# Attention scores in the scans' PSUM during a wait, and first expert products between the routing's steps

## The chip, the cores and the metric

The kernel runs on one core of one Trainium2 chip. The metric is the device time of one execution in microseconds (us), lower is better; the time of a kernel is the median of its runs.

## The reference

Four images of 32x32 pixels with 256 channels (1024 tokens each) pass through four layers. Cut to what matters here:

```python
# layer 0: norm, w_in to 512, depthwise 3x3 conv, gelu = x; then a selective scan, N = 64 states per channel
dA = exp(dtt[:, :, None] * A)                          # over the tokens of an image, one after the other
h  = dA * h + (dtt * xt)[:, :, None] * Bt[:, None, :]
y  = einsum('bdn,bn->bd', h, Ct)                       # then norm, w_out, residual
# layer 1: 1x1, grouped 3x3 and 1x1 convolution with batch norm and relu, residual
# layer 2: t + attention(norm(t)): 8 heads of 32; tokens see each other where edge_index has an edge
scores = where(mask, Q @ K.T / sqrt(32), -inf); attended = softmax(scores) @ V   # @ Wo, residual, norm
#          then t + mixture of 8 experts (hidden 256) on x = norm(t), which adds x itself:
probs  = softmax(x @ router);  weights = top2(probs) / their sum
out    = x + sum over e of weights[:, e] * (gelu(x @ w1[e] + b1[e]) @ w2[e] + b2[e])
# layer 3: t + gated scan(norm(t)): 512 channels, 16 states, the same recurrence
#          then t + mixture of 8 experts (hidden 512) on x = norm(t), top 2 without renormalisation
```

## The kernel before, in words

**The scans.** The two scan layers are cut into 1280 units of 128 partitions (channel and state) by 1024 tokens. `scans()` (line 351) emits them in the order of `SCANS`: layer 0 of image 0, layer 0 of image 1, layer 3 of image 0, and so on; the last three are layer 0 of image 3, written (0,3), then (3,2) and (3,3). A scan of layer 0 has 256 units, one of layer 3 has 64; each falls into four blocks `d` of 128 channels. One unit needs, under these names:

- `load`: SyncE loads of the row of time steps, broadcast into `dA` (2 DMAs with 64 states, 8 with 16);
- `decay`: ScalarE's exp over `dA`;
- `first`: two TensorE products that spread the inputs over the states into PSUM (`ps_rep`);
- VectorE's multiply of `ps_rep` by B (TENSOR_TENSOR), then the scan itself (TENSOR_TENSOR_SCAN into `h`);
- GpSimd's multiply of `h` by C, and per two units `pair`: eight TensorE products that sum over the states (`ps_y`).

`chunk(k)` brings the inputs of a new block (`S`, loaded from `parts` in DRAM) twelve units ahead (`AHEAD`); `chunks_ahead` may put it off until five units ahead (`LATEST`), and then calls `need`, which advances the other work until the block's `parts` are there.

**The stages.** Everything else is a list of generators: `front` b (up to the scan of layer 0), `middle` b (`back0`: the end of layer 0; layer 1; `attention`; `moe(2, ...)`; `front3`: the projections ahead of the scan of layer 3), `last` b (`back3`, `moe(3, ...)`, output). `run()` (line 535) advances the running stage by at most two steps after each half of a unit, and only while a hand-made meter of engine costs (`Metered`) says that no engine's sum is ahead of VectorE's. Where `need` advances, there is no such limit, and nothing of the scans is emitted meanwhile. The order in which instructions are emitted is each engine's order: no scheduler rearranges it, and an instruction that waits holds all behind it on its engine. Scan (3,3) is the one that waits: its first block needs all of `middle` 3, which may only begin when (0,3) is done. At that point unit 1210 is finished, and unit 1211 stands behind the wait.

**PSUM.** The scans have tag `x` (two buffers of two banks, for `ps_rep`) and `y` (one bank). The stages have tags `s` (two banks) and `acc` (one); `ps()` deals these three out in turn.

**Pipes.** `pipe` (line 179) puts steps of successive items behind one another in one emission order:

```python
    for tick in range(len(items) + len(steps) - 1):
        for s in reversed(range(len(steps))):
            if 0 <= tick - s < len(items):
                steps[s](items[tick - s])
                if cut and s:
                    yield cost
        yield cost if tick < len(items) else 0.5
```

So the later step of an older item is emitted ahead of the first step of the next one.

**Attention.** `heads` (line 1302) works on two heads and 512 queries. For each of eight blocks of 128 keys, `scores` makes two tiles `ps_sc` of 128x512 (six products: two of queries and keys, two of `mT`, a shift that is added, two of the mask with an identity), then two exps into `p`; `values` takes four products out of `p` into `ps_at` (two with the values, two with ones for the sums). An image has eight such calls, in two halves `nh` with four pairs of heads `hp` each. After a half come the division, `projected` and `normed`.

**Experts.** `moe` (line 1412): norm, transposes (`ps_tr`), logits `ps_lg`, then `route` on VectorE: largest logit, exp on ScalarE, sum, division, the best and second best expert; its result is `cw`, one weight per token and expert. `cw` is transposed (`ps_ct`), copied, multiplied by the second biases (`ps_b2`, written ps_b in the profile) and added to `tb`. Then the experts: a pipe with `one` (a product `ps_h`, or `ps_e`) and `two` (the Gelu of `ps_h` into `h_m`, or the accumulation of `ps_e` times `cw` into `tb`). `KH` is the number of hidden blocks of 128: 2 in layer 2, 4 in layer 3. ScalarE's functions live in tables, so an exp after a Gelu is preceded by a table load (ACT_TABLE_LOAD).

All instructions of these functions are recorded at one helper line (L124 of the meter), so the profile tells them apart by their tiles.

Of the kernel before, what the change touches and what calls it, by code (L numbers as in the profile page):

```python
# [7 lines left out]
F32 = mybir.dt.float32  # L8
BF16 = mybir.dt.bfloat16
I32 = mybir.dt.int32  # L10
AF = mybir.ActivationFunctionType
ALU = mybir.AluOpType
# [4 lines left out]
P = 128  # L17
NB = 4
L = 1024
TB = L // P  # L20
C = 256
# [3 lines left out]
NEXP = 8  # L25
# [16 lines left out]
AHEAD = 12  # L42
LATEST = 5
# [89 lines left out]
class Hybrid:  # L133
# [217 lines left out]
    def scans(self, mp, psum):  # L351
# [7 lines left out]
        nc = self.nc  # L359
        units = []  # L360
# [5 lines left out]
            ]  # L366
        chunks, rows, waiting = {}, {}, []
        state = {}
        y = None

        def chunk(k):
# [22 lines left out]
                )  # L394
            chunks[scan, d] = S

        def chunks_ahead(k):

            if k + AHEAD < len(units) and units[k + AHEAD][2:] == (0, 0, 0):
                waiting.append(k + AHEAD)  # L400
            while waiting:
                scan, d = units[waiting[0]][:2]
                if waiting[0] - k > LATEST and ("parts", *scan, d) not in self.ready:
                    break
                chunk(waiting.pop(0))

        def load(k):
            if k >= len(units):
# [70 lines left out]
        decay(1)  # L479
        first(0)  # L480
        for k in range(len(units) + 4):
            chunks_ahead(k)
            load(k + 4)
            first(k + 1)
            decay(k + 2)
            if k < len(units):
                a, inp = state.pop(k)
                B, Cm = rows[units[k][0]]
                nc.vector.tensor_tensor(inp, inp, B, ALU.mult)
            yield  # L490
            if k < len(units):
                h = mp.tile([P, L], F32, tag="h", name="h", bufs=5)
                nc.vector.tensor_tensor_scan(h, a, inp, 0.0, ALU.mult, ALU.add)
                nc.gpsimd.tensor_tensor(h, h, Cm, ALU.mult)
                state[k] = h
            if k % 2 == 1 and 2 <= k < len(units) + 2:
                pair(k - 2)
            yield

    def need(self, scan, d):  # L500
# [34 lines left out]
    def run(self):  # L535

        self.done, self.ready = set(), set()
        self.todo, self.stage, self.wait = list(STAGES), None, None
        nc, tc = self.nc, self.tc
        with tc.tile_pool(name="scan", bufs=1) as mp, tc.tile_pool(  # L540
            name="scps", bufs=1, space=PSUM
# [760 lines left out]
    def heads(self, fp, raw, sums, qT, kT, v, maskT, mT, nh, hp):  # L1302

        nc = self.nc
        qs = slice(nh * 512, (nh + 1) * 512)
        c, at = hp // 2, 64 * (hp % 2)
        acc = self.psum.tile([P, 512], F32, tag="acc", name="ps_at", bufs=1)
        got = {}  # L1310

        def scores(kb):
            two = [self.psum.tile([P, 512], F32, tag="s", name="ps_sc", bufs=2) for _ in range(2)]
            rows = [slice(at + 32 * i, at + 32 * i + 32) for i in range(2)]
            for i in range(2):
                nc.tensor.matmul(
                    two[i], lhsT=kT[rows[i], c, kb * P : (kb + 1) * P], rhs=qT[rows[i], c, qs],
                    start=True, stop=False,
                )
            for i in range(2):  # L1320
                nc.tensor.matmul(
                    two[i], lhsT=self.onesb[rows[i], :], rhs=mT[rows[i], c, qs],
                    start=False, stop=False,
                )
            for i in range(2):
                nc.tensor.matmul(
                    two[i], lhsT=self.identb, rhs=maskT[:, kb, qs], start=False, stop=True
                )
            got[kb] = p = fp.tile([P, 2, 512], F32, tag="p", name="p", bufs=3)
            for i in range(2):  # L1330
                nc.scalar.activation(p[:, i, :], two[i], AF.Exp)

# [8 lines left out]
                    start=(kb == 0), stop=(kb == TB - 1), tile_position=(0, 32 * i),  # L1341
                )

        yield from self.pipe(range(TB), scores, values, cost=1.3, cut=True)
        nc.scalar.copy(raw[at : at + 64, c, :], acc[:64, :])
        nc.scalar.copy(sums[at : at + 64, c, :], acc[64:, :])

# [64 lines left out]
    def moe(self, which, b, tb):  # L1412

        nc, tc, a = self.nc, self.tc, self.a
# [4 lines left out]
        KH = hidden // P  # L1419
        with tc.tile_pool(name=f"m{which}{b}", bufs=1, side="right") as op:  # L1420
# [11 lines left out]
            with tc.tile_pool(name=f"mg{which}{b}", bufs=1, side="right") as gp:  # L1432
# [5 lines left out]
                for j in range(TB):  # L1438
                    for k in range(2):
# [1 line left out]
                            ps[:, j, :], lhsT=xT[:, k, j * P : (j + 1) * P],  # L1441
                            rhs=self.router[which][:, k, :], start=(k == 0), stop=(k == 1),
                        )
                yield 3.0
                if which == 2:
                    nc.vector.tensor_copy(lg, ps)
                else:
                    nc.vector.tensor_tensor(
                        lg, ps, self.gb.unsqueeze(1).to_broadcast([P, TB, NEXP]), ALU.add
                    )  # L1450
                yield 0.5
                if which == 2:
                    for j in range(0, TB, 2):
                        tj = tb[:, j : j + 2, :]
                        nc.gpsimd.tensor_tensor(tj, tj, xn[:, j : j + 2, :], ALU.add)
                        yield 0.6
                yield from self.route(gp, lg, cw, which == 2)

                cT = gp.tile([NEXP, L], F32, name="cT")

                def turn(g):
                    ps = self.ps("ps_ct")
                    for k in range(4):
                        nc.tensor.transpose(
                            ps[:NEXP, k * P : (k + 1) * P], cw[:, 4 * g + k, :], self.ident
                        )
                    nc.scalar.copy(cT[:, g * 512 : (g + 1) * 512], ps[:NEXP, :])

                yield from self.pipe(range(2), turn, cost=0.8)
                got = {}  # L1470

                def last(j):
                    got[j] = ps = self.ps("ps_b2", (P, 2, C))
                    for i in range(2):
                        m = 2 * j + i
                        nc.tensor.matmul(
                            ps[:, i, :], lhsT=cT[:, m * P : (m + 1) * P], rhs=self.b2[which],
                            start=True, stop=True,
                        )

                def add(j):
                    tj = tb[:, 2 * j : 2 * j + 2, :]
                    nc.vector.tensor_tensor(tj, got.pop(j), tj, ALU.add)

                yield from self.pipe(range(TB // 2), last, add, cost=1.0)

            hidden_of = {}
            got = {}

            def one(item):  # L1490
                kind, e, g, i = item
                we1, we2 = weights[e]
                if kind == "h":
                    if i == 0:
                        hidden_of[e, g] = op.tile([P, KH, 512], F32, tag="h", name="h_m", bufs=2)
                        if g == 1 and e + 1 < NEXP:
                            weights[e + 1] = expert_weights(e + 1)
                    got[item] = ps = self.ps("ps_h")
                    self.mm(
                        ps, lambda k: we1[:, k, i * P : (i + 1) * P], xT, 2,  # L1500
                        slice(g * 512, (g + 1) * 512),
                    )
                    return
                h = hidden_of[e, g]
                got[item] = ps = self.ps("ps_e", (P, 2, C))
                for s in range(2):
                    m = 2 * i + s
                    for f in range(KH):
                        nc.tensor.matmul(
                            ps[:, s, :], lhsT=h[:, f, m * P : (m + 1) * P], rhs=we2[:, f, :],  # L1510
                            start=(f == 0), stop=(f == KH - 1),
                        )

            def two(item):
                kind, e, g, i = item
                if kind == "h":
                    nc.scalar.activation(
                        hidden_of[e, g][:, i, :], got.pop(item), AF.Gelu,
                        bias=b1[:, e * KH + i : e * KH + i + 1],
                    )  # L1520
                    return
                ps = got.pop(item)
                for s in range(2):
                    m = 4 * g + 2 * i + s
                    nc.vector.scalar_tensor_tensor(
                        tb[:, m, :], ps[:, s, :], cw[:, m, e : e + 1], tb[:, m, :],
                        ALU.mult, ALU.add,
                    )

            items = []  # L1530
            blocks = [(e, g) for e in range(NEXP) for g in range(2)]
            for n in range(len(blocks) + 1):
                if n < len(blocks):
                    items += [("h", *blocks[n], i) for i in range(KH)]
                if n:
                    items += [("o", *blocks[n - 1], i) for i in range(2)]
            yield from self.pipe(items, one, two, cost=2.6 if which == 2 else 3.4)

    def route(self, gp, lg, cw, renorm):

# [277 lines left out]
```

## Time and profile before

| | |
|---|---|
| runs | 6815.66, 6822.12, 6823.56 us; median 6822.12 |
| profiled execution | 6818.64 us; its span 6816.9 |
| mean granted TensorE clock | 0.828 |
| busy | PE 5387.2 us (79%), DVE 5225.0 (77%), POOL 3651.6 (54%), ACT 3449.8 (51%) |
| scans on VectorE | 1280 multiplies of 1213 ns mean, 1280 scans of 2285 ns |
| GpSimd's multiply | 1280 of 2372 ns |
| ACT_TABLE_LOAD | 495 of 1283 ns |
| DMA | 937.44 MB, 137 GB/s over the span |

The profile is one execution, taken by the hardware profiler. PE is TensorE's products, PEld its weight loads, DVE is VectorE, ACT ScalarE, POOL GpSimd, SP SyncE. A row of digits cuts the span into 40 slices of 170 us, each digit the busy tenths of a slice. A timeline row has the start in us, the length, the engine, the operation, output<-input, the shape, and in brackets the idle time before it and the instruction that ended it; "x4" joins neighbours of one kind. Times inside the span are counted from its start.

### The profile page before, as it was taken

How to read it: one execution, taken by the hardware profiler on the slowest of the kernel's cores; microseconds unless marked ns; L12 is line 12 of the kernel's file. 1: busy time of each engine (PE TensorE's matmuls, PEld its weight loads, DVE VectorE, ACT ScalarE, POOL GpSimd, SP SyncE). 2: the span in 40 equal slices, each digit the busy share in tenths (PEclk: the TensorE clock that was granted, in tenths of full speed). 3: DMA queues.
4: the chain of work that ended last, by engine and by line, in shares of the span. 5: the costliest groups of instructions: out<-in, count | busy, mean ns of one | idle time of the engine just before them, and what ended most of it. 6: DMA issues, size and time to landing. Idle time of an engine off the chain costs nothing. (4 is left out here: it accounts for less than half of the span.)

```text
span 6816.9 us, 65916 instructions
## 1 busy us (share of the span) xinstructions
PE 5387.2 (79%) x20320; PEld 2164.2 (32%) x20320; DVE 5225.0 (77%) x4486; ACT 3449.8 (51%) x4152; POOL 3651.6 (54%) x1801
## 2 busy tenths in 40 slices
PE   6558778579797568979689679798698687967979
PEld 3003213122242022234145222243253222523556
DVE  8778988988798987889889977798899861247411
ACT  2426666445476334557568345477485443245411
POOL 0876786755457655555856555557666540054200
PEclk8558779689798578979789689798698789877989
DMA  2556665754365665446756655366666640146321
GB/s 72 147 144 161 178 173 154 194 138 119 102 169 162 182 156 143 115 120 177 192 144 163 178 150 129 103 161 169 171 170 178 155 117 7 45 134 148 84 62 34
DMA packets 394235, 937.44 MB, mean 138 GB/s; under 512 B 83220, under 2 KB 165728, under 8 KB 392224
## 3 DMA queue, kind: packets, MB, share of 16 engines
q1 hardware_dynamic: 391696, 930.53, 51.3%
q8 instruction: 172, 2.82, 0.2%
q0 software_dynamic: 2128, 2.13, 0.2%
q14 instruction: 239, 1.96, 0.1%
HBM read 842.59 MB, written 93.95 MB: 137 GB/s over the span
## 5 line engine op out<-in xcount | busy, mean ns | idle before, releaser
L124 POOL TENSOR_TENSOR h<-h,rows 128x1024 f32<-128x1024 f32 x1280 | 3032.7, 2372 | 1995.8 <-DVE h L124 1649.5
L124 DVE TENSOR_TENSOR_SCAN h<-dA,ps_rep 128x1024 f32<-128x1024 f32 x1280 | 2925.3, 2285 | 238.9 <-issue 105.6
L124 DVE TENSOR_TENSOR ps_rep<-ps_rep,rows 128x1024 f32<-128x1024 f32 x1280 | 1552.9, 1213 | 289.0 <-PE ps_rep L124 288.8
L124 ACT ACTIVATE dA<-dA,A_L_conv_A_log 128x1024 f32<-128x1024 f32 x1024 | 1153.5, 1145 | 727.9 <-DMA dA<-dt 673.5
L124 PE MATMUL ps_rep<-S,spread_L_conv_A_log 96*128 96x512 bf16 x2048 | 765.6, 465 | 743.6 <-DVE h L124 710.4
L124 PE MATMUL ps_y<-h,collect_L_conv_A_log 128*32 128x512 f32 x4096 | 802.2, 761 | 95.5 <-POOL h L124 93.5
L124 PE MATMUL ps_h<-xTm,we 128*128 128x512 f32 x1536 | 719.0, 607 | 3.8 <-ACT h_m L124 2.2
L124 PE MATMUL ps_e<-we,h_m 128*128 128x256 f32 x3072 | 702.3, 381 | 8.1 <-ACT h_m L124 6.4
L124 ACT ACT_TABLE_LOAD x495 | 635.1, 1283 | 74.8 <-PE ps_h L124 44.3
L124 PEld LDWEIGHTS <-spread_L_conv_A_log 96*128 96x128 bf16 x2048 | 161.5, 103 | 1523.6 <-DVE h L124 1220.7
L124 PEld LDWEIGHTS ps_e<-we,h_m 128*128 128x128 f32 x3072 | 581.3, 190 | 155.4 <-issue 45.7
L124 ACT ACTIVATE p<-ps_sc 128x512 f32<-128x512 f32 x512 | 277.8, 594 | 549.9 <-PE ps_sc L124 537.4
L124 DVE SCALAR_TENSOR_TENSOR tb<-ps_e,cw,tb 128x256 f32<-128x256 f32 x512 | 220.6, 474 | 404.3 <-PE ps_e L124 404.3
L124 ACT ACTIVATE h_m<-ps_h,cols 128x512 f32<-128x512 f32 x384 | 260.7, 687 | 473.6 <-PE ps_h L124 470.9
L124 ACT ACTIVATE dA<-dA,A_L_attn_A_log 128x1024 f32<-128x1024 f32 x256 | 293.3, 1148 | 384.8 <-DMA dA<-dt 342.8
L124 PE MATMUL ps_at<-p,v 128*32 128x512 f32 x1024 | 374.6, 610 | 64.6 <-ACT p L124 53.8
L124 PEld LDWEIGHTS ps_h<-xTm,we 128*128 128x128 f32 x1536 | 291.7, 193 | 341.4 <-issue 294.2
L124 PE MATMUL ps_rep<-S,spread_L_attn_A_log 96*128 96x512 bf16 x512 | 184.4, 449 | 195.2 <-DVE h L124 177.1
L124 PE MATMUL ps_sc<-qT,kT 32*128 32x512 f32 x1024 | 295.2, 649 | 44.8 <-ACTq L1234 26.0
L124 PE MATMUL ps_at<-p,ones 128*32 128x512 f32 x1024 | 272.1, 610 | 0.0
L124 PEld LDWEIGHTS ps_y<-h,collect_L_conv_A_log 128*32 128x32 f32 x4096 | 107.4, 119 | 492.4 <-POOL h L124 243.3
L124 PE MATMUL ps_cv<-pad,diag 128*128 128x512 f32 x576 | 260.4, 593 | 0.0
(306 smaller groups left out, 4945.8 us busy)
## 6 DMA issues: line engine op xcount, KB each, us to landing
dA<-dt SPq DMA_DIRECT2D x2048, 256.0 KB
dA<-dt SPq DMA_DIRECT2D x2048, 64.0 KB
we<-in_L_ffn_W_dram SPq DMA_DIRECT2D x64, 512.0 KB
parts<-parts SPq DMA_DIRECT2D x64, 384.0 KB
S<-parts SPq DMA_DIRECT2D x96, 256.0 KB
dt<-sp_r SPq DMA_DIRECT2D x64, 256.0 KB
y<-yo SPq DMA_DIRECT2D x128, 128.0 KB
y_back<-y SPq DMA_DIRECT2D x64, 256.0 KB
```

The lines of the kernel that those rows point to most:

```text
L124: return got(*args, **kw)
```

## The change

It has two parts.

*Heads during the wait.* `chunks_ahead(k)` now returns True where the block's parts are not there. In that case `first(k + 1)` is left out at its usual place, unit k's multiply and scan are emitted first, and then `chunks_ahead(k, True)` waits with `self.alone` set, followed by `first(k + 1)`. A call of `heads` that begins while `self.alone` is set takes its score tiles from the scans' PSUM (tag `x`: both tiles of a block in one buffer, `ps_sx`), computes one exp of 128x1024 in place of two of 128x512, and its pipe has an empty step between scores and values, so that the values of a block are emitted after the scores of two blocks later.

*Routing.* In `moe`, all between `ps_lg` and the experts becomes a generator `routing()`. After each of its yields, one tick of the experts' pipe is emitted, for the first `2 * KH` ticks: eight in layer 3, four in layer 2. `one` and `two` are as they were.

```diff
@@ scans
-        def chunks_ahead(k):
-            if k + AHEAD < len(units) and units[k + AHEAD][2:] == (0, 0, 0):
+        def chunks_ahead(k, late=False):
+            if not late and k + AHEAD < len(units) and units[k + AHEAD][2:] == (0, 0, 0):
                 waiting.append(k + AHEAD)
             while waiting:
                 scan, d = units[waiting[0]][:2]
-                if waiting[0] - k > LATEST and ("parts", *scan, d) not in self.ready:
-                    break
+                if ("parts", *scan, d) not in self.ready:
+                    if waiting[0] - k > LATEST:
+                        break
+                    if not late:
+                        return True
+                    self.alone = True
                 chunk(waiting.pop(0))
+                self.alone = False
+            return False
...
         for k in range(len(units) + 4):
-            chunks_ahead(k)
+            waits = chunks_ahead(k)
             load(k + 4)
-            first(k + 1)
+            if not waits:
+                first(k + 1)
             decay(k + 2)
...
             if k % 2 == 1 and 2 <= k < len(units) + 2:
                 pair(k - 2)
+            if waits:
+                chunks_ahead(k, True)
+                first(k + 1)
             yield
@@ heads
+        alone = self.alone
...
-            two = [self.psum.tile([P, 512], F32, tag="s", name="ps_sc", bufs=2) for _ in range(2)]
+            if alone:
+                both = self.scan_psum.tile([P, 2, 512], F32, tag="x", name="ps_sx", bufs=2)
+                two = [both[:, i, :] for i in range(2)]
+            else:
+                two = [self.psum.tile([P, 512], F32, tag="s", name="ps_sc", bufs=2) for _ in range(2)]
...
+            if alone:
+                nc.scalar.activation(p, both, AF.Exp)
+                return
             for i in range(2):
                 nc.scalar.activation(p[:, i, :], two[i], AF.Exp)
...
-        yield from self.pipe(range(TB), scores, values, cost=1.3, cut=True)
+        if alone:
+            yield from self.pipe(range(TB), scores, lambda kb: None, values, cost=1.3)
+        else:
+            yield from self.pipe(range(TB), scores, values, cost=1.3, cut=True)
@@ moe
+                def routing():
+                    yield 3.0
...
+                    yield from self.route(gp, lg, cw, which == 2)
...
+                    yield from self.pipe(range(TB // 2), last, add, cost=1.0)
...
-            yield from self.pipe(items, one, two, cost=2.6 if which == 2 else 3.4)
+                experts = self.pipe(items, one, two, cost=2.6 if which == 2 else 3.4)
+
+                ahead = 2 * KH
+                for cost in routing():
+                    yield cost
+                    if ahead:
+                        ahead -= 1
+                        yield next(experts)
+            yield from experts
```

More of the change, by code (lines that the diff above doesn't have):

```diff
@@ L368, in scans @@
         state = {}
+        self.scan_psum = psum
         y = None
@@ L538, in run @@
         self.todo, self.stage, self.wait = list(STAGES), None, None
+        self.alone = False
         nc, tc = self.nc, self.tc
@@ L1324, in scores @@
                 )
+            got[kb] = p = fp.tile([P, 2, 512], F32, tag="p", name="p", bufs=3)
             for i in range(2):
@@ L1328, in scores @@
                 )
-            got[kb] = p = fp.tile([P, 2, 512], F32, tag="p", name="p", bufs=3)
+            if alone:
+                nc.scalar.activation(p, both, AF.Exp)
+                return
             for i in range(2):
@@ L1443, in moe @@
                         )
[L1444 to L1465, printed above, removed]
-                        )
-                    nc.scalar.copy(cT[:, g * 512 : (g + 1) * 512], ps[:NEXP, :])
-                yield from self.pipe(range(2), turn, cost=0.8)
@@ L1470, in moe @@
-                got = {}
[L1472 to L1478, printed above, removed]
-                        )
-                def add(j):
-                    tj = tb[:, 2 * j : 2 * j + 2, :]
-                    nc.vector.tensor_tensor(tj, got.pop(j), tj, ALU.add)
@@ L1485, in moe @@
[L1485 to L1511, printed above, removed]
-                        )
@@ L1514, in two @@
[L1514 to L1536, printed above, removed]
-            yield from self.pipe(items, one, two, cost=2.6 if which == 2 else 3.4)
+                def routing():
+                    yield 3.0
+                    if which == 2:
+                        nc.vector.tensor_copy(lg, ps)
+                    else:
+                        nc.vector.tensor_tensor(
+                            lg, ps, self.gb.unsqueeze(1).to_broadcast([P, TB, NEXP]), ALU.add
+                        )
+                    yield 0.5
+                    if which == 2:
+                        for j in range(0, TB, 2):
+                            tj = tb[:, j : j + 2, :]
+                            nc.gpsimd.tensor_tensor(tj, tj, xn[:, j : j + 2, :], ALU.add)
+                            yield 0.6
+                    yield from self.route(gp, lg, cw, which == 2)
+                    cT = gp.tile([NEXP, L], F32, name="cT")
+                    def turn(g):
+                        ps = self.ps("ps_ct")
+                        for k in range(4):
+                            nc.tensor.transpose(
+                                ps[:NEXP, k * P : (k + 1) * P], cw[:, 4 * g + k, :], self.ident
+                            )
+                        nc.scalar.copy(cT[:, g * 512 : (g + 1) * 512], ps[:NEXP, :])
+                    yield from self.pipe(range(2), turn, cost=0.8)
+                    got = {}
+                    def last(j):
+                        got[j] = ps = self.ps("ps_b2", (P, 2, C))
+                        for i in range(2):
+                            m = 2 * j + i
+                            nc.tensor.matmul(
+                                ps[:, i, :], lhsT=cT[:, m * P : (m + 1) * P], rhs=self.b2[which],
+                                start=True, stop=True,
+                            )
+                    def add(j):
+                        tj = tb[:, 2 * j : 2 * j + 2, :]
+                        nc.vector.tensor_tensor(tj, got.pop(j), tj, ALU.add)
+                    yield from self.pipe(range(TB // 2), last, add, cost=1.0)
@@ new lines, in moe, with one @@
+                hidden_of = {}
+                got = {}
+                def one(item):
+                    kind, e, g, i = item
+                    we1, we2 = weights[e]
+                    if kind == "h":
+                        if i == 0:
+                            hidden_of[e, g] = op.tile([P, KH, 512], F32, tag="h", name="h_m", bufs=2)
+                            if g == 1 and e + 1 < NEXP:
+                                weights[e + 1] = expert_weights(e + 1)
+                        got[item] = ps = self.ps("ps_h")
+                        self.mm(
+                            ps, lambda k: we1[:, k, i * P : (i + 1) * P], xT, 2,
+                            slice(g * 512, (g + 1) * 512),
+                        )
+                        return
+                    h = hidden_of[e, g]
+                    got[item] = ps = self.ps("ps_e", (P, 2, C))
+                    for s in range(2):
+                        m = 2 * i + s
+                        for f in range(KH):
+                            nc.tensor.matmul(
+                                ps[:, s, :], lhsT=h[:, f, m * P : (m + 1) * P], rhs=we2[:, f, :],
+                                start=(f == 0), stop=(f == KH - 1),
+                            )
@@ new lines, in two @@
+                def two(item):
+                    kind, e, g, i = item
+                    if kind == "h":
+                        nc.scalar.activation(
+                            hidden_of[e, g][:, i, :], got.pop(item), AF.Gelu,
+                            bias=b1[:, e * KH + i : e * KH + i + 1],
+                        )
+                        return
+                    ps = got.pop(item)
+                    for s in range(2):
+                        m = 4 * g + 2 * i + s
+                        nc.vector.scalar_tensor_tensor(
+                            tb[:, m, :], ps[:, s, :], cw[:, m, e : e + 1], tb[:, m, :],
+                            ALU.mult, ALU.add,
+                        )
@@ new lines, in moe @@
+                items = []
+                blocks = [(e, g) for e in range(NEXP) for g in range(2)]
+                for n in range(len(blocks) + 1):
+                    if n < len(blocks):
+                        items += [("h", *blocks[n], i) for i in range(KH)]
+                    if n:
+                        items += [("o", *blocks[n - 1], i) for i in range(2)]
+                experts = self.pipe(items, one, two, cost=2.6 if which == 2 else 3.4)
[5 more added lines that the diff above has]
+                        yield next(experts)
```

## The prediction

> **What bounds the kernel now.** I read the page first: engine totals and slices.
>
> ```profile
> span 6816.9 us, 65916 instructions
> ...
> PE 5387.2 (79%) x20320; PEld 2164.2 (32%) x20320; DVE 5225.0 (77%) x4486; ACT 3449.8 (51%) x4152; POOL 3651.6 (54%) x1801
> ...
> DVE  8778988988798987889889977798899861247411
> ```
>
> VectorE (the scans: 1280 units of a 1.21 us multiply and a 2.29 us scan) carries the program for 32 of 40 slices; then its digits fall to 1 and 2. What bounds that end is read from windows cut at its events: image 3's last five head pairs (their first ends its predecessor's copy at 5607.14), the rest of its middle stage, the last 69 scan units, the rest of image 2's last experts, and image 3's last stage.
>
> ```profile
> 5440.00:5608.00 168.00, 140.38 (x660) 41.24 (x659) 116.46 (x73) 77.45 (x107) 87.28 (x42) 0.90 0.51 130
> 5608.00:5768.00 160.00, 137.68 (x656) 34.85 (x652) 11.40 (x19) 53.52 (x99) 7.55 (x6) 1.00 0.00 1
> 5768.00:6048.00 280.00, 234.53 (x696) 134.19 (x697) 61.23 (x163) 95.17 (x146) 34.67 (x28) 0.89 0.15 50
> 6048.00:6380.00 332.00, 239.04 (x862) 106.99 (x861) 266.59 (x217) 172.85 (x182) 191.07 (x94) 0.75 0.63 162
> 6380.00:6515.00 135.00, 129.27 (x468) 86.76 (x464) 17.51 (x40) 25.14 (x36) 2.25 (x1) 0.99 0.11 34
> 6515.00:6817.00 302.00, 261.87 (x904) 176.48 (x904) 42.74 (x113) 53.35 (x82) 14.81 (x12) 0.89 0.17 51
> ```
>
> Columns: length, then PE, PEld, DVE, ACT, POOL busy, granted clock, DMA share, GB/s. In the second row VectorE works 11 of 160 us: scan (3,3) waits for this attention, so every microsecond here moves the end by one. The timeline of one key block shows what TensorE waits for:
>
> ```profile
> 5645.90 1.13 PE L124 MATMUL ps_sc<-qT,kT 32*128 32x512 f32 x4
> ...
> 5646.87 0.38 PE L124 MATMUL ps_sc<-mT,onesb 32*128 32x512 bf16 x2
> 5647.18 0.61 PE L124 MATMUL ps_sc<-maskT,identb 128*128 128x512 bf16 x2
> 5647.67 1.08 ACT L124 ACTIVATE p<-ps_sc 128x512 f32<-128x512 f32 x2 [2.80 <-PE ps_sc L124]
> ...
> 5648.32 1.10 PE L124 MATMUL ps_at<-p,v 128*32 128x512 f32 x3 [0.53 <-ACT p L124]
> 5648.80 0.11 PEld L124 LDWEIGHTS ps_at<-p,v 128*32 128x32 f32 x1 [0.35 <-ACT p L124]
> ...
> 5649.79 1.13 PE L124 MATMUL ps_sc<-qT,kT 32*128 32x512 f32 x4
> ```
>
> Scores, exp and values run one after the other, 3.89 us a block. TensorE waits twice: for the first head's exp (to 5648.32) and for the second's (5648.80). The other place is the chain of waits in the last routing:
>
> ```profile
> 6567.22 6.64 PE ps_lg L124 x32
> ...
> 6573.88 0.24 DVE lg L124
> ...
> 6579.36 1.86 PE ps_ct L124 x8
> 6581.23 7.12 PE ps_b L124 x16
> 6588.35 15.49 PE ps_h L124 x32
> ```
>
> TensorE stands still for the 5.5 us of VectorE's steps and comes back slow: 32 ps_h take 15.49 us, 16 of them later 6.87 us, so 1.75 us is start-up, about four instructions at 0.85 instead of 0.43.
>
> **The change part by part.** My sum is against the profiled execution, 6818.64 us (its span of 6816.9 and 1.7 around it). That is 3.5 below the median of 6822.12, inside the three runs' own spread, so I correct nothing for it.
>
> *Heads in the scans' PSUM.* The wait is raised once, for scan (3,3): image 3's last five pairs, 40 blocks. In the built order their values follow the scores of two blocks later, and one exp of 128x1024 replaces two of 128x512. So the values' input is ready. Step by step from the timeline: scores 0.97 (5645.90 to 5646.87), mT 0.31, mask 0.44 (5566.29 to the next product at 5566.73), values 0.99. That last is the nearest row, ps_y, same shape (128*32, eight instructions):
>
> ```profile
> 6335.73 0.43 PE ps_rep L124 x2
> 6336.16 0.99 PE ps_y L124 x8
> ```
>
> Sum 2.71, so 1.18 saved a block, 40 x 1.18 = 47. ScalarE's exp (two were 1.08; the 128x1024 decay takes 1.15) fits under 2.71; were TensorE faster than that, it would be the bound. Given back: the last values of a pair wait some 0.35 for their exp (5 x 0.35 = 1.8), and in pair (1,2) the copies of the sums wait behind a table load, two small activations and four of 0.52 (about 2). **-43.** Bounds: only the recorded 0.53 goes (21), or nothing is given back (48). A rule speaks against the 47: the Trainium skill, TensorEngine Tiling (Array Packing), Key Properties, says that a change of tiling mode, not just of tile, drains TensorE, and mask to values is such a change, twice a block. By it the 0.53 may be drain; if all of it stayed the part would give 26, with the second wait alone 20. But ps_rep to ps_y above is the same change from full columns to 32-column tiles, and ps_y starts with no gap and takes 0.99 with its drain. I take the row.
>
> *Scan unit 1211 ahead of the wait.* Its multiply and scan (3.5 us) move from behind the stretch into its idle VectorE, its eight dA loads too (8 x 0.46 on SP). first(1212) is late next, but needs only 0.43 to 1.0 us while VectorE still has sp_x work. **-3.5** (0 to -6).
>
> *First products between the routing steps.* Eight for the last experts (KH 4), four for the middle ones.
> Tail (image 3): in the built order seven products stand before ps_ct. From the end of ps_lg: first product cold 3.4, six more 10.3 (4 x 0.43 each), ps_ct half 0.5, eighth 1.7, ps_ct 0.5, ps_b at full clock half of 7.12, 3.6: about 20.5. Now 6573.86 to 6603.84 is 30.0. The routing's exp now queues behind one Gelu and two table loads (3.4 + 0.7 + 1.3: at 5.7 instead of 0.8), cw is ready near 10, still before 13.7. **-9.5** (-4 to -11).
> Image 3's middle experts: only four products, three Gelus ahead of the exp on ScalarE. Products end at 8.6; exp at 3.4 + 1.7 + 1.7 + 0.7 + 1.3 + 0.3 = 9.2; five more us of VectorE: ps_ct at 14.3 instead of 6.3. ps_e starts at 14.3 + 1.8 + 7.1 = 23.3 instead of 24.15, and cold (1.7). **+1** (-3 to +3): the idle only changes place. Here a second rule counts: the Trainium skill, ScalarE: Activation LUTs, What ACT_TABLE_LOAD costs, gives about 1283 ns and a drain of about 1380. The profile's 495 loads have mean 1283, and at 6243.12 a decay starts as the load from 6241.83 ends: no drain. By the rule this routing costs 1.4 more; the whole built order has twenty more loads, 26 us of ScalarE by the row, 53 by the rule, nearly all beside VectorE's work.
> Image 2's last experts (scan units 1243 to 1247): VectorE idle 51 - 36.24 = 14.8 in 6205 to 6256, mostly for ps_rep and ps_b behind cold products. I take 3 off; and the stage stands one unit further at the last scan, a fifth of a 13.8 us expert half, 2.8. **-6** (-12 to +4).
> The five routings earlier: VectorE idles 10.6 + 10.3 + 11.0 + 12.4 + 12.1 = 56 in the same windows; the products now sit where TensorE waited for cw. No row shows the new mixture. Best, half of it goes (-28); worst, half of the added loads is exposed (+13). I take **-8**, near the middle.
> Moved with them: the second expert's two weight loads (0.4 us each on SP), now ahead of some dA loads. Their buffer is free, so they block none. Gpsimd's tb adds keep their place among its h multiplies. The fourth product needs the first one's PSUM, freed by its Gelu at 4.2. Behind the waiting exp on ScalarE stand the next decays, needed two units later by a scan.
>
> Sum: -43 - 3.5 - 9.5 + 1 - 6 - 8 = -69, so **6750 us**.
>
> **The rivals.**
> A, the drain stays: heads save 20 instead of 43, **6773**. For it the rule and the changes of mode; against it ps_y's 0.99.
> B, the routings give more: TensorE stays at full clock through ps_ct and ps_b and half of the 56 us goes: 20 more, **6730**. For it the granted clock of 0.56 to 0.68 there; against it that in the middle experts the four products are used up before the steps begin.
> C, slower, by ScalarE's order in the six routings under the scans: r_sm on VectorE waits for the exp, that for Gelus (3 x 3 in the middle experts, 3 x 1 in the last: 12), these for products that stand behind ps_rep, which waits for VectorE's scan. Price at most 3.4 + 0.7 + 2 x 1.28 + 0.26 = 6.9 each, 83 us, in place of the -8: **6841**. It eats the other gains (61) from 5.1 us a Gelu. Against it: the built order puts two scan units between lg and r_mx, and ScalarE waited 7 to 9 us for lg there.
> D, that the change does nothing, is excluded for the heads by the built order (40 exps of 128x1024); that gains and stalls cancel stays: about 6818.
>
> **How the numbers follow.** 0.2% (13.6 us) is about what a measurement of this kernel can tell from no change. Forecast 65% (6725 to 6772), A 16%, B 12%, C 4%, D 3%. The range of 6715 to 6785 leaves out C, D and the far ends of A and B. Faster 0.93 (forecast, A, B), same 0.03, slower 0.04.
>
> **What would show it.** In the profile after: blocks of ps_sx with 2.7 us from one to the next (3.4 would be A), no idle before ps_at; the last five pairs in about 116 us instead of 159.3; 20 us from ps_lg's end to the first ps_e in the tail; in image 3's middle routing a TensorE idle of 5 to 6 us before ps_ct, as before; VectorE idle per earlier routing at or below 10 us (above 15 is C). I am wrong if the heads keep 3.9 us, or units in the routings get longer.

## The result, and the profile after

The changed kernel takes 6789.42 us (median of 5 runs, 6779.12 to 6801.22) where the kernel before takes 6822.12; the ratio is 0.9958, 95% interval 0.9944 to 0.9972. It is faster by 0.4%, some 29 us, where 69 were forecast. Its profiled execution took 6789.42 us, so the profile stands at the median. The page:

```profile
span 6787.7 us, 65819 instructions
...
PE 5341.0 (79%) x20236; PEld 2153.2 (32%) x20320; DVE 5226.4 (77%) x4486; ACT 3474.5 (51%) x4132; POOL 3650.6 (54%) x1801
...
DVE  8778988988798997789889987888899872237511
```

VectorE's digits hardly differ from before over the first 32 slices (five of them by one, up or down); in the wait a 1 has become a 2. The windows of the end, cut at the same events as before (columns: length, then PE, PEld, DVE, ACT, POOL busy, granted clock, DMA share, GB/s):

```profile
5636.00:5760.00 124.00, 118.93 (x642) 30.08 (x650) 11.08 (x18) 50.08 (x57) 7.54 (x6) 0.96 0.00 1
5760.00:6041.00 281.00, 235.51 (x690) 135.06 (x690) 61.14 (x162) 95.91 (x146) 32.88 (x27) 0.89 0.15 48
6041.00:6364.00 323.00, 236.05 (x875) 108.68 (x876) 267.06 (x215) 177.96 (x189) 190.23 (x95) 0.78 0.67 166
6364.00:6494.00 130.00, 124.12 (x451) 83.91 (x449) 17.52 (x40) 23.86 (x34) 2.27 (x1) 0.99 0.12 35
6494.00:6788.00 294.00, 260.49 (x904) 175.63 (x904) 42.75 (x113) 55.63 (x84) 14.80 (x12) 0.91 0.17 52
```

The rows were 160, 280, 332, 135 and 302 us long before. So the end of the program gained far more than 29 us, and the first window now begins 28 us later than before: that much was lost ahead of the wait. Event by event, after minus before, from the starts in the two traces:

| event | before | after | difference |
|---|---|---|---|
| scan of unit 1210, the last ahead of the wait | 5592.1 | 5619.7 | +27.6 |
| copy behind the last head pair (`sums`) | 5767.06 | 5759.77 | -7.3 |
| image 3's middle experts, first `ps_e` | 5828.3 | 5821.9 | -6.4 |
| image 3's last stage, first product (`ps_o`) | 6526.1 | 6504.8 | -21.3 |
| image 3's last experts, first `ps_e` | 6603.84 | 6572.78 | -31.1 |
| end of the span | 6816.9 | 6787.7 | -29.2 |

The heads gained 34.9, image 2's last experts and the scan units beside them 14.9, the tail's routing 9.8; the stretch ahead of all this, up to unit 1210, lost 27.6. VectorE, the bound of that stretch, has no more work in it: the windows from the start to that unit's scan, of the kernel before and of the changed one (columns as above):

```profile
0.00:5592.13 5592.13, 4370.67 (x16670) 1621.39 (x16670) 4823.24 (x3936) 3042.97 (x3597) 3398.40 (x1660) 0.82 0.57 152
0.00:5619.69 5619.69, 4351.02 (x16597) 1615.95 (x16670) 4821.08 (x3936) 3062.88 (x3611) 3397.70 (x1660) 0.82 0.58 151
```

The same 3936 instructions take 4821.1 us instead of 4823.2. All of the loss is waiting of VectorE; the units did not get longer (multiply and scan have means of 1213 and 2285 ns, as before). The timeline of one key block in the wait shows the heads' part (engine, operation, output<-input, shape, and in brackets the idle time before and what ended it):

```profile
5639.19 1.13 PE L124 MATMUL ps_sx<-qT,kT 32*128 32x512 f32 x4
...
5640.16 0.38 PE L124 MATMUL ps_sx<-mT,onesb 32*128 32x512 bf16 x2
...
5640.47 0.60 PE L124 MATMUL ps_sx<-maskT,identb 128*128 128x512 bf16 x2
...
5641.01 0.62 PE L124 MATMUL ps_at<-p,v 128*32 128x512 f32 x2
...
5641.17 1.02 ACT L124 ACTIVATE p<-ps_sx 128x1024 f32<-128x1024 f32 x1 [1.78 <-PE ps_sx L124]
...
5642.00 0.70 PE L124 MATMUL ps_sx<-qT,kT 32*128 32x512 f32 x2
```

A block is 2.81 us (5639.19 to 5642.00) instead of 3.89. TensorE waits for nothing; ScalarE's one exp lies beside the values of an older block, and ScalarE waits 1.78 for TensorE. The chain of waits in the tail shows the routing's part:

```profile
6545.49 6.63 PE ps_lg L124 x32
6552.12 14.42 PE ps_h L124 x28
6566.54 0.44 PE ps_ct L124 x4
6566.98 1.72 PE ps_h L124 x4
6568.69 0.44 PE ps_ct L124 x4
6569.13 3.65 PE ps_b L124 x16
6572.78 8.79 PE ps_e L124 x32
```

Before, nineteen small VectorE steps and one exp stood in this chain. Now it holds TensorE alone, `ps_ct` comes at full clock, and `ps_b` takes 3.65 us instead of 7.12. From the end of `ps_lg` to the first `ps_e` it is 20.7 us instead of 30.0.

### The profile page after: what moved, and what is told of

It reads as the page before. It is cut to its first block, busy times and chain, and to the rows that moved or that the text cites. A ratio compares the mean times of both kernels' runs of the same rounds, so it can differ in the third digit from the quotient of the medians.

```text
span 6787.7 us, 65819 instructions
## 1 busy us (share of the span) xinstructions
PE 5341.0 (79%) x20236; PEld 2153.2 (32%) x20320; DVE 5226.4 (77%) x4486; ACT 3474.5 (51%) x4132; POOL 3650.6 (54%) x1801
## 5 line engine op out<-in xcount | busy, mean ns | idle before, releaser
L124 DVE TENSOR_TENSOR_SCAN h<-dA,ps_rep 128x1024 f32<-128x1024 f32 x1280 | 2925.4, 2285 | 231.6 <-issue 97.3
L124 DVE TENSOR_TENSOR ps_rep<-ps_rep,rows 128x1024 f32<-128x1024 f32 x1280 | 1553.1, 1213 | 269.5 <-PE ps_rep L124 268.9
L124 ACT ACTIVATE p<-ps_sc 128x512 f32<-128x512 f32 x432 | 234.4, 594 | 451.2 <-PE ps_sc L124 289.7
L124 PE MATMUL ps_at<-p,v 128*32 128x512 f32 x1024 | 357.0, 615 | 45.9 <-ACT p L124 35.1
L124 PE MATMUL ps_sc<-qT,kT 32*128 32x512 f32 x864 | 251.3, 653 | 43.8 <-ACTq L1248 36.1
```

Of the source, the lines that this page charges most:

```text
L124: return got(*args, **kw)
```

## The experiments

The times of four groups of runs, each on a chip of its own, are compared by their ratio to the kernel before on the same chip (its medians there: 6818.34, 6813.90, 6822.28 and 6812.29). "Unit 1210" is how much later than before that unit's scan starts in the one profiled execution. Five of these kernels (heads alone, late routing, two exps, norm on VectorE, only where free) have the order of the kernel before up to there, and read -2.4, +1.8, -5.9, -7.1 and +1.6: so a shift of some 7 us is what one execution can show with no change of order.

| kernel | median us | ratio (95%) | unit 1210 |
|---|---|---|---|
| heads alone | 6780.36 | 0.9947 (0.9933 to 0.9960) | -2.4 |
| routing alone | 6827.02 | 1.0012 (1.0006 to 1.0019) | +25.9 |
| heads, late routing | 6757.50 | 0.9907 (0.9893 to 0.9921) | +1.8 |
| heads, last experts' routing | 6768.98 | 0.9918 (0.9903 to 0.9933) | +11.0 |
| changed, exp first | 6756.16 | 0.9908 (0.9894 to 0.9922) | +6.3 |
| changed, Gelu early | 6771.86 | 0.9942 (0.9929 to 0.9956) | -0.9 |
| heads alone, two exps | 6777.65 | 0.9948 (0.9935 to 0.9962) | -5.9 |
| late routing, norm on VectorE | 6747.05 | 0.9902 (0.9887 to 0.9917) | -7.1 |
| changed, exp first and Gelu early | 6762.44 | 0.9917 (0.9901 to 0.9932) | +6.7 |
| exp first, norm on VectorE | 6756.15 | 0.9905 (0.9886 to 0.9923) | +2.3 |
| only where free, norm on VectorE | 6751.21 | 0.9900 (0.9882 to 0.9918) | +1.6 |
| changed kernel again | 6780.29 | 0.9941 (0.9927 to 0.9955) | +28.2 |
| heads, middle experts 0 to 2 only | 6794.29 | 0.9976 (0.9967 to 0.9985) | +9.4 |
| heads, last experts 0 and 1 only | 6782.71 | 0.9959 (0.9945 to 0.9972) | +4.7 |

**Which part loses.** The heads' part alone has `moe` as before; the routing alone has the changed `moe` and `heads` and `scans` as before. The next two keep the heads and restrict the early products:

```diff
-                ahead = 2 * KH
+                ahead = 2 * KH if which == 3 and b >= 2 else 0     # late routing
+                ahead = 2 * KH if which == 3 else 0                # last experts' routing
```

> The heads' part as in the changed kernel (with unit 1211 ahead of the wait), the routing as before. Theory (the new routing order costs under the scans and gains in the tail, about +7 us together): about 6784 us, that is -38 against before (five pairs -35, unit 1211 -3), with the scans' starts up to unit 1210 where they were before. Rival (the 27.6 us lost ahead of the wait come from the heads' part, by a change of program size or of tile positions): unit 1210's scan again about 28 us later than before, and the total at 6810 or above.

> The routing of the changed kernel, the heads as before. Theory: unit 1210's scan 20 to 30 us later than before, image 2's last experts and the tail 20 us earlier; total about 6829 us, slower than before by 0.1%. Rival (the loss ahead of the wait was a chance of that one execution): unit 1210 within 5 us of before and a total near 6800.

> Heads as in the changed kernel; first products between the routing's steps only in the last experts of images 2 and 3, none in the five routings ahead of the wait nor in image 3's middle experts. Theory: the 27.6 us ahead of the wait come back, the rest stays: about 6760 us, 29 below the changed kernel. Rival (chance): as the changed kernel, about 6789.

> Heads as in the changed kernel; first products between the routing's steps in the last experts of all four images (8 each), none in the middle experts. Theory that the middle experts' order carries most of the loss (idle of VectorE +5.4, +5.9, +8.3 us in their three windows): about 20 less than the changed kernel, 6768. Rival that the last experts' order carries as much (slip of 9 and 4.5 us around the routings of images 0 and 1): 6780 or more.

All four came out as the theory had them, within 4 us. The routing alone makes the kernel slower, although the tail's 9 us are in it. Its unit 1210 is 25.9 later, in the changed kernel 27.6, in a second execution of it 28.2: this is no chance of one execution. Left out of the routings under the scans, the loss is gone, and the kernel is at 0.9907.

> The changed kernel once more, beside the other three on one chip. Theory: unit 1210's scan again 20 to 30 us later than before, in a second execution, and the same total, 6780 to 6795. Rival (chance): within 5 us of before at unit 1210 and a total near 6765.

**What in the middle experts loses.** The timeline of the changed kernel in image 2's middle experts, between `lg` and the products by the biases:

```profile
4428.55 1.28 ACT L124 ACT_TABLE_LOAD   x1
4429.84 0.69 ACT L124 ACTIVATE h_m<-ps_h,cols 128x512 f32<-128x512 f32 x1
4430.55 1.28 ACT L124 ACT_TABLE_LOAD   x1
4431.84 1.15 ACT L124 ACTIVATE dA<-dA,A_L_conv_A_log 128x1024 f32<-128x1024 f32 x1
4432.90 0.24 ACT L124 ACTIVATE lg<-lg 128x64 f32<-128x64 f32 x1
...
4433.17 0.22 DVE L124 TENSOR_REDUCE r_sm<-lg 128x8 f32<-128x64 f32 x1 [2.84 <-ACT lg L124]
...
4443.41 1.86 PE L124 MATMUL ps_ct<-ident,cw 128*8 128x128 f32 x8 [6.24 <-DVE cw L124]
...
4449.29 0.69 ACT L124 ACTIVATE h_m<-ps_h,cols 128x512 f32<-128x512 f32 x1
4450.03 2.07 PE L124 MATMUL ps_b<-b,cT 8*128 8x256 f32 x4 [4.75 <-ACT h_m L124]
...
4452.20 0.69 DVE L124 TENSOR_TENSOR tb<-ps_b,tb 128x512 f32<-128x512 f32 x1 [5.62 <-PE ps_b L124]
```

Two new waits are seen here, neither in the trace of before. First, the routing's exp stands behind the third Gelu, two table loads and a decay on ScalarE; VectorE waits 2.84 us for it. Second, the first `ps_b` waits 4.75 us for the fourth Gelu. They share no data: the three PSUM buffers are dealt out in turn, and after the fourth `ps_h` come two `ps_ct`, so that the first `ps_b` gets the fourth product's buffer. That product's Gelu belongs to the pipe's fifth tick, which is emitted only behind the whole routing; on ScalarE it stands behind two decays and a table load. VectorE then stands 5.62 us for `ps_b`, with a scan unit queued behind. The groups of VectorE in this window show the sum, of the changed kernel and then of the kernel before (busy, mean ns | idle before, and for what):

```profile
L124 DVE TENSOR_TENSOR tb<-ps_b,tb 128x512 f32<-128x512 f32 x4 | 2.7, 685 | 10.0 <-PE ps_b L124 10.0
```

```profile
L124 DVE TENSOR_TENSOR tb<-ps_b,tb 128x512 f32<-128x512 f32 x4 | 2.7, 682 | 4.2 <-PE ps_b L124 4.2
```

Each wait was taken away by itself, in the middle experts of all images, by an order that avoids it. "Exp first" starts the early products after the seventh of the routing's steps, the one that emits the exp. "Gelu early" puts the first four products and Gelus in a pipe of their own, with a fifth tick for the last Gelu:

```diff
+                for n, cost in enumerate(routing()):               # exp first
...
-                    if ahead:
+                    if ahead and (which == 3 or n >= 6):
```

```diff
+                if which == 2:                                     # Gelu early
+                    early = self.pipe(items[: 2 * KH], one, two, cost=cost)
+                    experts = self.pipe(items[2 * KH :], one, two, cost=cost)
...
-                ahead = 2 * KH
+                ahead = 2 * KH + (which == 2)
...
-                        yield next(experts)
+                        yield next(early)
```

> The changed kernel, but in the middle experts the four early products begin only after the step that emits the routing's exp. Theory that the exp queued behind Gelus and table loads is what costs there (idle of VectorE for lg 0.3 + 4.2 + 2.8 us, 9.6 in image 3's): 7 us back ahead of the wait and some 7 in image 3's middle experts, about 6775. Rival that the loss is in the products by the biases (ps_b idle 10 us more than before in the three windows), which this leaves: 6785 to 6790.

> The changed kernel, but in the middle experts the fourth early product's Gelu is emitted one routing step after it and not behind the routing, so that the first ps_b finds its PSUM buffer free. Theory that ps_b waits for that Gelu through the shared PSUM (4.8 us of TensorE idle in image 2's window, 0 in the other two): 5 to 10 us back, about 6782, and no idle of TensorE with the releaser h_m. Rival that the Gelu's place is a detail, and one more Gelu ahead of the exp costs as much: 6787 to 6793.

> The changed kernel with both edits in the middle experts: early products only after the routing's exp, and the fourth Gelu ahead of the transposes of cw. Theory that the exp behind the Gelus and the ps_b behind the last Gelu are two separate losses: what each alone gave adds up, exp first -33 and Gelu early another 10 or so, about 6745. Rival that they are two ways to remove the same loss (the early products put the routing out of step with the scan units): no better than exp first alone, 6754 to 6760.

By the ratios exp first gained 0.50% (34 us) on the changed kernel's first measurement and 0.33% (23 us) on its second, where 14 us were expected. The two profiled executions lie 33 us apart. In image 3's middle experts, where no scan runs, it does what was meant, and TensorE's stop is gone. The timeline of that kernel there:

```profile
5772.65 0.26 ACT L124 ACTIVATE lg<-lg 128x64 f32<-128x64 f32 x1 [6.81 <-DVE lg L124]
...
5780.38 1.04 PE L124 MATMUL ps_ct<-ident,cw 128*8 128x128 f32 x8
...
5782.12 3.99 PE L124 MATMUL ps_b<-b,cT 8*128 8x256 f32 x16 [0.70 <-ACT cT L124]
...
5786.03 4.23 PE L124 MATMUL ps_e<-we,h_m 128*128 128x256 f32 x12
```

From the first `ps_lg` to the first `ps_e` it takes 21.0 us there against 32.0 in the changed kernel (31.0 before). The other two thirds lie ahead of the wait: unit 1210 at +6.3 and, with the norm's edit, +2.3.

Gelu early is less clear. Its total (0.9942) is 0.16% (11 us) below the changed kernel's first measurement and equal to its second (0.9941), so a gain is not shown by the totals. In its trace unit 1210 is at -0.9, but that execution was 10 us faster than its median. No `ps_b` of a middle stage waits for a Gelu there, and VectorE's idle for `ps_b` in image 2's window is 4.2 again.

What VectorE waited for `ps_b` and for the exp, from the start to unit 1210 (us in total, times, longest), in the kernel before, in the changed one (two rows) and with exp first; where no row for the exp stands, VectorE did not wait for it:

```profile
DVE tb L124 <- PE ps_b L124: 17.0, 8, 2.4
```

```profile
DVE tb L124 <- PE ps_b L124: 33.9, 13, 5.6
DVE r_sm L124 <- ACT lg L124: 7.4, 3, 4.2
```

```profile
DVE tb L124 <- PE ps_b L124: 19.6, 8, 7.0
```

The two waits grew by 24 us together; beside them VectorE's wait for `ps_e` grew by 8 and that for `ps_rep` fell by 14. Exp first takes away the wait for the exp and most of the added wait for `ps_b`, though the buffer's wait is still in its trace of image 2's middle experts:

```profile
4438.71 7.19 PE L124 MATMUL ps_b<-b,cT 8*128 8x256 f32 x16 [4.89 <-ACT h_m L124]
```

VectorE then stands 7.04 us for `ps_b`, longer than in the changed kernel, and the kernel is as fast as with the late routing all the same. Both edits together are no better than exp first alone: the rival of that run is right. So starting the early products ahead of the exp is shown to carry most of the loss. What the buffer's wait costs by itself is not shown, nor how the 27 us divide. The added table loads are no rival: exp first keeps 8 of the 20, both edits together none, with no lower total.

**Which routings lose.** The last two runs have the heads' part, and early products only in the middle experts of images 0 to 2, or only in the last experts of images 0 and 1.

> Heads as changed; early products only in the middle experts of images 0, 1 and 2. Theory that these carry most of the loss: unit 1210 some 18 to 22 us later than before, total about 6800 (heads alone 6780 plus that). Rival that they carry half or less: unit 1210 at most 12 later, 6790.

> Heads as changed; early products only in the last experts of images 0 and 1. Theory that the middle experts carry most of the loss: unit 1210 3 to 8 us later than before, total about 6785. Rival that these two carry half or more: unit 1210 14 or more later, 6795.

Against the heads alone (0.9947) the middle experts cost 0.29% (20 us; 14 by the medians), the last ones 0.12% (8 us; 2 by the medians). The intervals (0.09 to 0.14% either way) are wide for this, and the first run's total (6794) lies between its theory and its rival. By the totals the middle experts carry about two thirds or more, and the sum is 16 to 28 us. By unit 1210 the two (+9.4 and +4.7, each known to some 7 us) make only half of the 27.6: +9.4 is what the rival had. That the parts add up is therefore not shown. Nor do the waits become delay one for one: with the middle experts of images 0 to 2 only, the two waits are 31.4 and 9.3 us, as long as in the changed kernel. In the last experts eight products cover all steps and the exp stands behind one Gelu, not three.

**The heads.** Does the gain come from the distance between scores and values, or from joining the exps?

```diff
-            if alone:
-                nc.scalar.activation(p, both, AF.Exp)
-                return
             for i in range(2):
                 nc.scalar.activation(p[:, i, :], two[i], AF.Exp)
```

> The heads' part alone (routing as before) with the scans' PSUM and the empty step, but two exps of 128x512 in place of one of 128x1024. Theory that only the distance between scores and values counts: blocks of 2.81 us as with one exp, total as in the heads alone, 6780. Rival that joining the exps carries part of the gain (ScalarE as the bound, or the second exp late for the values): blocks of 3.1 us or more, 6792 or above.

From the distance: two exps of 128x512 in place of one (1.08 us instead of 1.02 on ScalarE) give 0.9948 against 0.9947. The values follow two blocks behind the scores, and ScalarE has room for either.

More than half of what the heads gave less than the forecast lies in one place, the norm of the attention's first half. The timeline of the changed kernel there:

```profile
5708.06 2.08 ACT L124 ACTIVATE y_at<-y_at,lny_b,lny_r 128x256 f32<-128x256 f32 x4 [1.02 <-DVE lny_b L124]
...
5711.36 1.94 ACT L124 ACTIVATE p<-ps_sx 128x1024 f32<-128x1024 f32 x2
...
5712.44 0.62 PE L124 MATMUL ps_at<-p,v 128*32 128x512 f32 x2 [2.41 <-ACT p L124]
...
5713.43 2.02 PE L124 MATMUL ps_sx<-qT,kT 32*128 32x512 f32 x4
...
5716.77 1.07 PE L124 MATMUL ps_at<-p,v 128*32 128x512 f32 x2
...
5718.64 2.08 PE L124 MATMUL ps_sx<-qT,kT 32*128 32x512 f32 x4
...
5723.87 1.13 PE L124 MATMUL ps_sx<-qT,kT 32*128 32x512 f32 x4
```

The four activations and two copies stand ahead of two exps. TensorE waits 2.41 us and then runs at half its speed until 5723.87: 2.02 to 2.08 for the scores that else take 1.13, with a granted clock of 0.68 in the ten us from 5710 and 0.81 in the next ten, 1.00 around them. The pair with the norm takes 30.0 us, the next one 26.3, where the first two take 22.7. VectorE is idle there, so the norm was given to it:

```diff
+            if self.alone and tag == "lny":
+                nc.vector.tensor_scalar(
+                    out[:, j, :], src[:, j, :], r[:, j : j + 1], b[:, j : j + 1], ALU.mult, ALU.add
+                )
+            else:
                 nc.scalar.activation(
```

> Heads, and the new routing in the last experts of images 2 and 3 only (6757.5 before this edit); in addition the norm after the attention's first half, while the scan waits, is applied by VectorE and not by ScalarE (four of 128x256, 2.08 us on ScalarE). Theory that these four held up two exps, so that TensorE stood 2.4 us and then ran at the lower clock for some ten us: the pair with the norm takes 27 instead of 30.0 us and the next one 22.7 instead of 26.3 to 27.4, total about 6750. Rival that ScalarE's table load and the copies ahead of it hold the exps anyway: no more than 2 us, 6755 to 6758.

> Exp first in the middle experts (6756.2 before this edit) and the attention's norm applied by VectorE during the wait. Theory: the two act in different stretches and add: -8 us as in the run that had the norm alone (alone stretch 117.2 instead of 125.5), about 6748. Rival: 6754 or more.

> Early products only where few or no scan units run beside the routing: image 3's middle experts (exp first) and the last experts of images 2 and 3; heads as changed, norm on VectorE; the five early routings as in the kernel before. Theory (early products pay where VectorE is idle and cost where it is the bound): the run with late routing and norm was 6747, image 3's middle routing gives another 11 (first ps_e 21 us after ps_lg begins instead of 31): about 6737, the lowest of all. Rival (exp first pays under the scans too): this is no better than the exp-first kernel with the norm.

The pair with the norm then takes 27.0 us and the next one 22.1; the five pairs are 117.2 us long instead of 125.5 with the late routing. The timeline of the late routing with the norm on VectorE:

```profile
5673.37 2.33 DVE L124 TENSOR_SCALAR y_at<-y_at,lny_r,lny_b 128x256 f32<-128x256 f32 x4
5673.45 1.13 PE L124 MATMUL ps_sx<-qT,kT 32*128 32x512 f32 x4
5673.56 1.02 ACT L124 ACTIVATE p<-ps_sx 128x1024 f32<-128x1024 f32 x1
...
5675.26 0.62 PE L124 MATMUL ps_at<-p,v 128*32 128x512 f32 x2
```

TensorE waits for no exp. In the totals this is hardly to be seen: 0.9902 against 0.9907 for the late routing, and 0.9905 against 0.9908 with exp first (that run missed its 6748 by 8; its rival, 6754 or more, came true). Early products in image 3's middle experts too ("only where free") brought their 9 us in the trace (22.0 from the first `ps_lg` to the first `ps_e`, 31.2 without), but no clearly lower total: 0.9900, and 6751 where 6737 was expected; unit 1210 lay 8.7 us later in that execution than in the one without. All five of these versions (late routing and exp first, each with and without the norm on VectorE, and only where free) are faster than both kernels, by about 0.9 to 1.0% against the kernel before and some 0.3 to 0.6% against the changed one (0.9958 and 0.9941 in its two groups of runs); among themselves they can't be told apart.

## Why the prediction was wrong, step by step

- **The five routings ahead of the wait: the step that failed.** The forecast had -8 with bounds of -28 and +13; measured are +27.6, +25.9 and +28.2. The prediction took TensorE's wait for `cw` as free room. The room was there, but filling it put three Gelus with their table loads ahead of the routing's exp, and made the first `ps_b` wait for a Gelu emitted behind the routing. In place of the gain of 8 VectorE waited 24 us more, 7 for the exp and 17 for `ps_b`. Rival C had the first of these at 83 us in all, and the prediction argued it away with ScalarE's 7 to 9 us of waiting for `lg`; those were spent on the Gelus and their table loads (in the timeline above the exp follows them and one decay without a pause). By the prediction's own sign, VectorE's idle time per routing (10 or less, above 15 for C), the five routings have 13, 14, 11, 19 and 8 us: only image 2's middle experts read as C. The second wait was near at hand: the prediction said that the fourth product needs the first one's buffer, and did not ask who needs the fourth one's. The upper bound of +13 counted table loads as ScalarE's time, and left out that VectorE, the bound, queues scan units behind the steps that wait.
- **The heads: right in mechanism, -34.9 where -43 was forecast.** A block saves 1.08 us instead of 1.18 (2.81 against 2.71): mask to values takes 0.54 and not 0.44. That is 4 us of 40 blocks. The drain that rival A took from the Trainium skill (TensorEngine Tiling (Array Packing), Key Properties) can be no more than this 0.10 us at that change of tiling mode, and not 0.53. By the shapes a block has three such changes, not two; the other two take what the forecast had. The second rule, a drain behind each table load, is not seen: the Gelu at 4429.84 starts as the load from 4428.55 ends. A pair is 22.7 us, 0.2 more than eight blocks, where the forecast had 0.35. The norm cost 7.3 and 3.6 us in two pairs, 10.9 where before it cost 3.5; the forecast added about 2 for it and missed the half speed behind the gap.
- **Unit 1211: right.** Its scan starts at 5626.7 beside the heads, and unit 1212 is 7.4 us earlier than before, unit 1213 10.4, where the stage ahead of them is 6.4 earlier: 1 to 4 us, forecast 3.5.
- **Image 3's middle experts: right,** +1.0 (from -7.4 at the first `ps_lg` to -6.4 at the first `ps_e`), forecast +1. TensorE's idle before `ps_ct` is 5.8 us, as it was said to stay.
- **Image 2's last experts: better,** about -12 (14.9 less the 1 to 4 of unit 1211) where -6 was forecast with a bound of -12.
- **The tail: right,** -9.8 where -9.5 was forecast; 20.7 us from the end of `ps_lg` to the first `ps_e`, forecast 20.5 (the terms that the prediction lists add to 20.0). Some 2 us go back in the experts behind it.

The sum is 27.6 - 34.9 + 1 - 15 - 10 + 2 = -29. With the forecast's -8 in the first place it would be -65, so the miss of 40 is 36 from that one step and 8 from the heads, less some 5 that image 2's experts and unit 1211 gave above their forecast.

## What to carry to other kernels

Work put into one engine's waits was not free here, because engines that serve it had the bound's next step queued behind: count, per engine in its order, what stands ahead of the small step that everyone waits for, here an exp of 0.24 us. Where PSUM buffers go round, ask of each early product which later tile gets its buffer, and where its reader is emitted. And one change at many places is many changes: the same reordering gained 10 us in the tail, where VectorE was idle, and lost 27 where it was the bound.

## What was not expected of the hardware

A gap of 2.4 us on TensorE may or may not cost its clock. The same gap at the same place (2.40 or 2.41 us, at the norm) stands in ten of the traces. By the granted clock in them, TensorE runs at half speed beside it for no time at all (exp first), for 3.4 us (Gelu early and two others), 6.8 (the changed kernel again), 10.2 (the changed kernel and two others) or 13.7 (late routing and one other): always a multiple of 3.4. The pair behind the gap takes 21.5, 23.1, 24.7, 26.3 and 27.4 us in these, so one such gap spreads equal work by up to 6 us.

A small VectorE instruction can take as long as GpSimd's large one beside it. In image 2's routing of the changed kernel, with GpSimd's multiply running:

```profile
4436.23 2.42 POOL L124 TENSOR_TENSOR h<-h,rows 128x1024 f32<-128x1024 f32 x1 [3.54 <-DVE r_one_m L124]
4436.23 0.23 DVE L124 TENSOR_TENSOR r_one<-lg,r_one_m 128x64 f32<-128x64 f32 x1
4436.49 2.25 DVE L124 TENSOR_TENSOR r_one<-r_one,orderf 128x64 f32<-128x64 f32 x1
4438.77 0.22 DVE L124 TENSOR_REDUCE r_one_m<-r_one 128x8 f32<-128x64 f32 x1
```

The same form takes 0.22 us a few rows later (`r_two`), and in the same window `lg` less its largest took 2.28. Of the 88 such steps (TENSOR_TENSOR of 128x64) in this trace 14 take more than 0.5 us, 12 of 88 in the trace of before, and each of these ends within 0.15 us of the end of a GpSimd instruction. So where such a step falls beside GpSimd's work decides its price, up to tenfold. The prediction's sum had none of it, but it is not the loss: up to unit 1210 all of VectorE's 128x64 steps together take 3.7 us more than before, and its work as a whole 2 us less.
